# Two-layer transformer kernel: look-up transfers on ScalarE's queue, row marks copied at their own part, two groups of sends released at later parts

## The chip, the cores and the metric

The kernel runs on one core of a Trainium2 chip. The metric is device time in microseconds of one execution of the whole program; lower is better. Engines are named as in the profile: PE (TensorE, matmuls), DVE (VectorE), ACT (ScalarE), POOL (GpSimd), SP (SyncE, which here only issues DMAs).

## The reference, cut to what matters

Two layers are computed on 2 x 1024 tokens of width 512, all in float32: attention, a mixture of experts, a state-space layer and a feed-forward layer, each added to its input after a layer norm.

```
x = x + attention(layernorm(x))              # 16 heads
x = x + experts(layernorm(x))                # 32 experts, the best 8 of each token
x = x + state_space(layernorm(x))            # 16 heads, chunks of 64
x = x + look_up_ffn(layernorm(x))            # weights = lut[idx], 16 values

# experts, for every token t and each of its 8 experts e, with weight masked_w[t, e]:
h   = silu(x[t] @ w_gate[e].T) * (x[t] @ w_up[e].T)        # 192 wide
out[t] += masked_w[t, e] * (h @ w_down[e].T)

# look_up_ffn: gate_idx, up_idx [1376, 512], down_idx [512, 1376], integers 0 to 15
w = lut[idx]                                                # for each of the three
```

The change lies where the experts are computed. The look-up `w = lut[idx]` of the last layer's weights is done beside them.

## The kernel before, in words

**Routing and sends.** Every token's row (512 normalised values, its token number, and its 32 expert weights: `ROW` = 545 floats) is written once for each of its 8 experts into a table `rows` in HBM, at a place that belongs to the expert. A write is an indirect DMA on POOL of 128 rows (`send`, L296). Place k (0 to 7) of a token is its k-th expert, counted from the highest number down. Tokens of the first batch are sent during attention. Of the second batch some places are sent as soon as they are routed; the others come in groups, `send(k)` for place k: 2 DMAs for k = 1, 8 for each k from 2 to 7. Such a send also waits for the latest silu `self.first` of the experts (L1090).

**Parts.** The experts are done from number 31 down to 0, each in two parts: a front part (2 blocks of 128 rows) and a back part (3 blocks, which hold rows of the second batch too). The list `order` has the 64 parts: fronts of n = 0, 1, 2, backs of 0 and 1 (parts 3 and 4), and then front n, back n - 1 in turn (part 5 is front 3, part 6 back 2, part 7 front 4, and so on). `part(p)` writes the instructions of one part, with four yields:

1. `load_weights`, then `gates(p, 0)` (8 matmuls and a silu on ACT), then `begin_turn(p + 1)`;
2. `turn_block` 0 and 1 of part p + 1 (transposes of its rows, copied by ACT to `xgT`), then `down(p - 1)`;
3. `gates(p, 1)` (8 matmuls, a product `hT` on DVE);
4. `turn_block` 2 of part p + 1 (back parts only), `gates(p, 2)` (8 matmuls, silu on ACT, products `hU` on DVE), and `load_rows(p + 3)`.

`begin_turn(p + 1)` has the two copies of the row marks on DVE, L1060 and L1061: `rw` (the rows' weights for this expert) and `tok` (their token numbers), both with four buffers and both read from the rows `xg` (three buffers). They are used in `down`: ACT scales a block of the result by `rw` into `y` (L1140, six buffers), and POOL adds it to `acc` in HBM with an accumulating indirect DMA at the rows `tok` (L1142). `acc` has two halves, used in turn, and accumulations into the same half are kept in order.

**Look-up.** `_look_up` is a generator. It handles 27 pieces of 128 x 688 or 128 x 512 indices. For a piece, `load` fetches it (L921, issued on SP, two buffers), ACT casts it to bf16 (`shorten`, L926), and DVE goes through 16 steps: a compare (L942) and a multiply-add into `acc` (L943; step 0 is one instruction, L937). This `acc` is a tile of the look-up with two buffers, not the table of the experts. The next piece is loaded at step 1 and cast at step 14; the result is stored at step 15 (L951, issued on SP). One `next(look_up)` does one step. From part 5 on, `rest` calls it after each yield of a part: 6 steps in a front part, 9 in a back part.

**What sets the order.** PE, DVE and ACT run in the order in which the program is written (`manual_schedule`). The queues of POOL and SP are ordered by the framework's planner, from this order and its estimates. Each queue is issued in order, so an instruction that waits holds what is behind it.

**Where sends are released.** `rest` issues `send(0)` (empty), `send(1)` and `send(2)` before its loop, `send(3)` in part 2, and `send(4)` to `send(7)` in parts 5, 7, 9 and 11, each after the part's first yield.

Of the kernel before, what the change touches and what calls it, by code (L numbers as in the profile page):

```python
# [32 lines left out]
E, I, TOPK = 32, 192, 8  # L33
# [24 lines left out]
FI, NLUT = 1376, 16  # L58
# [264 lines left out]
def _after(tc, later, earlier, kind=mybir.DependencyClass.Sync):  # L323
    tc.add_manual_dep(
        later.ins, earlier.ins.name, mybir.DependencyInfo(kind, mybir.DependencyReason.DATA)
    )


def _attention(tc, g, x_sb, a, router, gates, load_gates, make_experts):
# [14 lines left out]
    with ExitStack() as ctx:  # L344
# [462 lines left out]
        def group(i, beside, sending):  # L807
# [49 lines left out]
            first, second = (fold(i + 1, hf) if follows else iter(()) for hf in range(2))  # L857
            next(first, None)
            next(ahead, None)
            run(first)  # L860
            next(second, None)
            one(len(blocks) - 1)
            for _ in range(2):
                next(ahead, None)
            run(second)
            run(ahead)
            next(division, None)

# [34 lines left out]
def _look_up(tc, g, a, pool, lut, ffn_w):  # L903

    nc = tc.nc
    half = FI // 2
    pieces = []
    for src, dst in (("gidx", "wg"), ("uidx", "wu")):  # L910
        for cc in range(NCC):
            for hf in range(2):
                cols = slice(hf * half, (hf + 1) * half)
                pieces.append((P, half, a[src][:, cc, cols], ffn_w[dst][:, cc, cols]))
    for fc in range(NFC - 1):
        pieces.append((P, D, a["didx"][:, fc, :], ffn_w["wd"][:, fc, :]))
    pieces.append((FTAIL, D, a["didx_tail"], ffn_w["wd_tail"]))

    def load(n, width, src, dst):
        idx = pool.tile([P, half], I32, tag="idx", name="idx", bufs=2)[:n, :width]  # L920
        nc.sync.dma_start(out=idx, in_=src)  # L921
        return idx

    def shorten(idx, n, width, src, dst):
        short = pool.tile([P, half], BF16, tag="short", name="short", bufs=2)[:n, :width]
        nc.scalar.copy(short, idx)  # L926
        return short

    idx = load(*pieces[0])
    yield  # L930
    short = shorten(idx, *pieces[0])
    for i, (n, width, src, dst) in enumerate(pieces):
        more = pieces[i + 1 : i + 2]
        acc = pool.tile([P, half], F32, tag="acc", name="acc", bufs=2)[:n, :width]
        for k in range(NLUT):
            if k == 0:
                nc.vector.tensor_scalar(  # L937
                    acc, short, float(k), lut[:n, k : k + 1], ALU.is_equal, ALU.mult
                )
            else:  # L940
                hit = pool.tile([P, half], BF16, tag="hit", name="hit", bufs=2)[:n, :width]
                nc.vector.tensor_scalar(hit, short, float(k), None, ALU.is_equal)  # L942
                nc.vector.scalar_tensor_tensor(  # L943
                    acc, hit, lut[:n, k : k + 1], acc, ALU.mult, ALU.add
                )
            if k == 1 and more:
                idx = load(*more[0])
            if k == NLUT - 2 and more:
                ahead = shorten(idx, *more[0])
            if k == NLUT - 1:  # L950
                nc.sync.dma_start(out=dst, in_=acc)  # L951
            yield
        if more:
            short = ahead


def _expert_gates(tc, a, loaded):
# [23 lines left out]
class _Experts:  # L981
# [70 lines left out]
    def begin_turn(self, p):  # L1052
        if p >= len(self.order):
            return
        nc, n, xg = self.tc.nc, self.blocks(p), self.xg[p]
        most = CAPB - FRONTB
        xgT = self.wk.tile([P, NCC, most * P], F32, tag="xgT", name="xgT", bufs=2)
        tok = self.wk.tile([P, most], U32, tag="tok", name="tok", bufs=4)[:, :n]
        rw = self.wk.tile([P, most], F32, tag="rw", name="rw", bufs=4)[:, :n]
        nc.vector.tensor_copy(rw, xg[:, :, D + 1 + self.expert(p)])  # L1060
        nc.vector.tensor_copy(tok, xg[:, :, D])  # L1061
        self.turned[p] = xgT, tok, rw

    def turn_block(self, p, j):
        if p >= len(self.order) or j >= self.blocks(p):
# [83 lines left out]
    def part(self, p):  # L1149

        back = self.order[p - 1] if p else (0, 0)
        if back[1]:
            self.load_weights(back[0] + 3)
        self.gates(p, 0)
        self.begin_turn(p + 1)
        yield
        for j in range(2):
            self.turn_block(p + 1, j)
        self.down(p - 1)
        yield  # L1160
        self.gates(p, 1)
        yield
        self.turn_block(p + 1, 2)
        self.gates(p, 2)
        self.load_rows(p + 3)
        yield

    def ahead(self):

        for n in range(2):  # L1170
            self.load_rows(n)
            self.load_weights(n)
        self.load_rows(2)
        self.load_weights(2)
        yield
        self.begin_turn(0)
        for j in range(2):
            self.turn_block(0, j)
        yield
        for p in range(2):  # L1180
            back = self.order[p]
            self.gates(p, 0)
            self.begin_turn(p + 1)
            yield
            for j in range(2):
                self.turn_block(p + 1, j)
            self.down(p - 1)
            yield
            self.gates(p, 1)
            yield  # L1190
            self.gates(p, 2)
            yield

    def rest(self, sends, fetch):

        tc, a = self.tc, self.a
        nc = tc.nc
        with ExitStack() as ctx:
            def pool(name, bufs, space=None):
                kw = {} if space is None else {"space": space}  # L1200
                return ctx.enter_context(
                    tc.tile_pool(name=name, bufs=bufs, reuse_waits="tile", **kw)
                )

            self.banks = {
                "g": (pool("se_ps_g", 2, PSUM), "g", 2),
                "t": (pool("se_ps_t", 2, PSUM), "t", 2),
                "o": (pool("se_ps_o", 2, PSUM), "o", 2),
                "m": (pool("se_ps_m", 1, PSUM), "m", 1),
            }  # L1210
            lk = pool("se_lk", 1)
            self.both = True

            def send(k):
                for routed, places in sends:
                    if places == [k]:
                        for _ in self.router.send(routed, places, self.first):
                            pass

            for k in range(3):  # L1220
                send(k)
            for p in (3, 4):
                self.load_rows(p)
            look_up = _look_up(tc, self.g, a, lk, self.g["lut"], self.ffn_w)
            next(look_up)
            for p in range(2, len(self.order)):
                n, back = self.order[p]
                for i, _ in enumerate(self.part(p)):
                    if i == 0 and not back and n + 1 < TOPK:

                        send(n + 1)
                    if p > 4:
                        for _ in range(1 + back + (i < 1 + (not back))):
                            next(look_up, None)
                if back and n >= TOPK:
                    got = next(fetch, None)
                    if got:
                        _after(tc, got, self.first)
            self.down(len(self.order) - 1)
            for _ in chain(look_up, fetch):  # L1240
                pass
# [718 lines left out]
```

## Time and profile before

| | |
|---|---|
| median of 3 runs | 2810.66 us (2804.3 to 2813.29) |
| profiled execution | 2820.1 us, its span 2818.4 us |
| mean granted TensorE clock | 0.982 |
| busy, share of the span | PE 96%, DVE 51%, ACT 33%, POOL 23% |
| DMA | 316 MB, mean 112 GB/s |
| experts with the look-up beside them | about 866 to 1535 us of the span |

The times in the trace are microseconds from the start of the span of the one profiled execution, on one core. A row of the timeline has the start, the duration, the engine, the line of the kernel, the operation, `out<-in` by the program's names with shapes, a count, and in brackets the idle time before it and what ended it. Busy time of an engine leaves out instructions that issue DMAs. A wait is put down to the releaser that came last by the profile.

### The profile page before, as it was taken

The numbers are of one execution on the slowest core, as the hardware profiler recorded it, in microseconds if no ns is written. First come the engines' busy times: TensorE is split into PE (matmuls) and PEld (weight loads), VectorE is DVE, ScalarE is ACT, GpSimd is POOL, SyncE is SP. The second block draws the span as 40 slices with busy tenths as digits, with TensorE's granted clock in tenths as the row PEclk, the third lists the DMA queues.
The fourth block names the chain that finished last, engine by engine and source line by source line (L and its number), as shares of the span: only waits on it lengthen the run. The fifth ranks groups of instructions, "written<-read, shape, count | busy, mean of one in ns | idle before, by whom it ended". The sixth has DMA issues, their size and how long they took to land. (4 is left out here: it accounts for less than half of the span.)

```text
span 2818.4 us, 34644 instructions
## 1 busy us (share of the span) xinstructions
PE 2703.1 (96%) x11976; PEld 1624.1 (58%) x11976; DVE 1425.4 (51%) x3952; ACT 933.1 (33%) x1887; POOL 635.7 (23%) x787
## 2 busy tenths in 40 slices
PE   7999999998989899999999699999999999999999
PEld 3444444544465566666665587777777775444444
DVE  5555543655236788987775344554455453101100
ACT  1344432443323233333333333443444433101010
POOL 2222220433355634333333000110111010000000
PEclk9999999998989999999999799999999999999999
DMA  3376532212479999998886301111111140100000
GB/s 115 111 199 184 164 115 70 92 60 74 153 247 248 241 228 255 263 240 202 205 205 107 84 16 36 38 41 44 28 47 42 35 147 20 34 8 27 30 0 26
DMA packets 242793, 315.60 MB, mean 112 GB/s; under 512 B 60753, under 2 KB 129361, under 8 KB 241841
## 3 DMA queue, kind: packets, MB, share of 16 engines
q1 hardware_dynamic: 208320, 234.87, 28.0%
q0 software_dynamic: 33280, 77.68, 13.1%
q8 instruction: 98, 1.61, 0.2%
q10 hardware_dynamic: 1008, 0.73, 0.1%
q14 instruction: 87, 0.70, 0.1%
HBM read 160.17 MB, written 153.04 MB: 111 GB/s over the span
## 5 line engine op out<-in xcount | busy, mean ns | idle before, releaser
L1080 PE MATMUL pg<-xgT,wgu 128*128 128x256 f32 (+1 forms) x1536 | 447.2, 444 | 13.8 <-DVE hT L1093 12.7
L1080 PEld LDWEIGHTS pg<-xgT,wgu 128*128 128x128 f32 x1536 | 289.0, 194 | 161.1 <-issue 51.2
L1142 POOL DMA_INDIRECT acc<-y,tok x160 | 272.9, 1706 | 401.8 <-ACT y L1140 186.7
L943 DVE SCALAR_TENSOR_TENSOR acc<-hit,lut,acc 128x688 f32<-128x688 bf16 (+2 forms) x405 | 348.8, 861 | 14.4
L1443 PE MATMUL pf<-xT,win 128*128 128x256 f32 x1024 | 242.5, 385 | 5.5 <-ACT gate L1471 3.8
L653 ACT ACTIVATE pT<-st 128x512 f32<-128x512 f32 (+3 forms) x384 | 158.7, 497 | 180.6 <-PE st L640 158.0
L548 PE MATMUL sp<-ka,qa 64*128 64x512 f32 (+3 forms) x768 | 207.3, 511 | 8.1 <-DVE mx L569 4.0
L1443 PEld LDWEIGHTS pf<-xT,win 128*128 128x128 f32 x1024 | 187.0, 190 | 38.8 <-PE pf L1443 7.2
L640 PE MATMUL st<-qa,ka 64*128 64x512 f32 (+3 forms) x768 | 182.4, 512 | 2.3 <-issue 1.5
L569 DVE TENSOR_REDUCE mx<-sp 128x1 f32<-128x384 f32 (+3 forms) x352 | 167.3, 492 | 17.4 <-PE sp L548 10.7
L657 POOL TENSOR_SCALAR_AFFINE_SELECT pT<-pT 128x128 f32<-128x128 f32 x256 | 83.5, 338 | 390.2 <-ACT pT L653 378.3
L296 POOL DMA_INDIRECT rows<-row,idx x128 | 128.7, 1005 | 108.3 <-DVE chosen L282 43.6
L1750 PE MATMUL po<-wd,f_hT 128*128 128x512 f32 (+1 forms) x352 | 152.6, 592 | 0.0
L671 PE MATMUL y<-pT,v 128*64 128x512 f32 (+3 forms) x768 | 145.7, 512 | 4.6 <-ACT raw L608 3.1
L562 DVE CUSTOM_DVE_ANT_0 junk<-sp,cmask 128x128 f32<-128x128 f32 x256 | 73.3, 286 | 145.3 <-PE sp L548 135.4
L548 PEld LDWEIGHTS sp<-ka,qa 64*128 64x128 f32 x768 | 91.8, 187 | 93.5 <-issue 49.7
L1694 DVE TENSOR_TENSOR f_hT<-s,pu 128x512 f32<-128x512 f32 (+1 forms) x37 | 25.5, 688 | 232.8 <-PE pu L1688 232.8
L640 PEld LDWEIGHTS st<-qa,ka 64*128 64x128 f32 x768 | 102.3, 192 | 63.2 <-issue 36.9
L1515 POOL TENSOR_TENSOR cd<-ft_c,ec 128x256 f32<-128x256 f32 x56 | 40.8, 730 | 413.3 <-PE cb L1529 205.2
L1140 ACT ACTIVATE y<-yo,rw 128x512 f32<-128x512 f32 x128 | 81.2, 684 | 157.9 <-PE yo L1133 150.1
L1443 PE MATMUL pf<-xT,wc 128*128 128x256 f32 x512 | 125.0, 391 | 8.8 <-DVE ft_b L1462 5.2
L1688 PE MATMUL pg<-f_xT,wg 128*128 128x512 f32 (+1 forms) x296 | 133.4, 593 | 0.0
(213 smaller groups left out, 4034.3 us busy)
## 6 DMA issues: line engine op xcount, KB each, us to landing
rows<-blank SPq DMA_DIRECT2D x160, 272.5 KB
xg<-rows SPq DMA_DIRECT2D x32, 817.5 KB
xg<-rows SPq DMA_DIRECT2D x32, 545.0 KB
csb<-cs_rows SPq DMA_DIRECT2D x128, 128.0 KB
wgu<-in_wg_dram SPq DMA_DIRECT2D x32, 256.0 KB
wgu<-in_wu_dram SPq DMA_DIRECT2D x32, 256.0 KB
wd<-in_wd_dram SPq DMA_DIRECT2D x32, 256.0 KB
wd<-in_wd_dram SPq DMA_DIRECT2D x64, 128.0 KB
```

The source lines that it names most:

```text
L296: t = tc.nc.gpsimd.indirect_dma_start(out=self.rows[:, :], out_offset=bass.IndirectOffsetOnAxis(ap=idx[:, i, k : k + 1], axis=0), in_=xr[i ...
L548: nc.tensor.matmul(sp[hh][:, c0:c1], lhsT=q[half, pr, tb * P : (tb + 1) * P], rhs=k[half, pr, k0 * P : k1 * P], start=True, stop=True,)
L569: nc.vector.tensor_reduce(m[:, n : n + 1], sp[hh][:, c0:c1], AX.X, ALU.max)
L640: nc.tensor.matmul(st[:, c0:], lhsT=k[half, j // 2, kb * P : (kb + 1) * P], rhs=q[half, j // 2, qt * 512 + c0 : (qt + 1) * 512], start=Tru ...
L653: e = nc.scalar.activation(pT[:, c0:], st[:, c0:], AF.Exp)
L671: nc.tensor.matmul(y[j // 2][half, c0:], lhsT=v[:, kb, h // 2, h % 2 : h % 2 + 2, :].rearrange("p k d -> p (k d)"), rhs=ps[j][:, c0:], sta ...
L943: nc.vector.scalar_tensor_tensor(acc, hit, lut[:n, k : k + 1], acc, ALU.mult, ALU.add)
L1080: nc.tensor.matmul(pg, lhsT=wgu[:, cc, m * P : (m + 1) * P], rhs=xgT[:, cc, :cols], start=cc == 0, stop=cc == NCC - 1,)
L1142: nc.gpsimd.indirect_dma_start(out=self.router.acc[to][:, :], out_offset=bass.IndirectOffsetOnAxis(ap=tok[:, j : j + 1], axis=0), in_=y, i ...
L1443: nc.tensor.matmul(pf, lhsT=w[wn][:, cc, c0 : c0 + P], rhs=xT[st][:, cc], start=cc == 0, stop=cc == NCC - 1,)
L1688: nc.tensor.matmul(dst[:n, :], lhsT=w[:, cc, fc * P : fc * P + n], rhs=self.xT[tt][:, cc, :], start=cc == 0, stop=cc == NCC - 1,)
L1750: nc.tensor.matmul(po, lhsT=self.hT[tt][fc // 4][:n, fc % 4, j * P : (j + 1) * P], rhs=wd[:n, fc, :], start=fc == 0, stop=fc == NFC - 1,)
```

## The change

Three things are changed, all in the experts' stage. (a) The loads and stores of the look-up are issued on ACT's queue instead of SP's, and a piece is stored at step 4 of the next piece instead of at its own last step; the last piece is stored after one more yield. (b) The two copies of the row marks leave `begin_turn(p + 1)` for a function `marks(p)` that `part(p)` and `ahead` call just before `begin_turn(p + 1)`; so the marks of a part are copied in its own part, not in the part before. (c) `send(2)` moves from before the loop to part 2, and `send(3)` from part 2 to part 3; `send(4)` to `send(7)` stay.

```diff
 def _look_up(tc, g, a, pool, lut, ffn_w):
     def load(n, width, src, dst):
         idx = pool.tile([P, half], I32, tag="idx", name="idx", bufs=2)[:n, :width]
-        nc.sync.dma_start(out=idx, in_=src)
+        nc.scalar.dma_start(out=idx, in_=src)
         return idx
...
+    done = None
     for i, (n, width, src, dst) in enumerate(pieces):
...
             if k == NLUT - 2 and more:
                 ahead = shorten(idx, *more[0])
-            if k == NLUT - 1:
-                nc.sync.dma_start(out=dst, in_=acc)
+            if k == 4 and done:
+                nc.scalar.dma_start(out=done[0], in_=done[1])
             yield
+        done = dst, acc
         if more:
             short = ahead
+    yield
+    nc.scalar.dma_start(out=done[0], in_=done[1])
...
     def begin_turn(self, p):
         if p >= len(self.order):
             return
-        nc, n, xg = self.tc.nc, self.blocks(p), self.xg[p]
+        n = self.blocks(p)
         most = CAPB - FRONTB
         xgT = self.wk.tile([P, NCC, most * P], F32, tag="xgT", name="xgT", bufs=2)
         tok = self.wk.tile([P, most], U32, tag="tok", name="tok", bufs=4)[:, :n]
         rw = self.wk.tile([P, most], F32, tag="rw", name="rw", bufs=4)[:, :n]
+        self.turned[p] = xgT, tok, rw
+
+    def marks(self, p):
+        nc, n, xg = self.tc.nc, self.blocks(p), self.xg[p]
+        _, tok, rw = self.turned[p]
         nc.vector.tensor_copy(rw, xg[:, :, D + 1 + self.expert(p)])
         nc.vector.tensor_copy(tok, xg[:, :, D])
-        self.turned[p] = xgT, tok, rw
...
         self.gates(p, 0)                 # in part(p), and alike in ahead()
+        self.marks(p)
         self.begin_turn(p + 1)
...
-            for k in range(3):
+            for k in range(2):
                 send(k)
...
                 for i, _ in enumerate(self.part(p)):
-                    if i == 0 and not back and n + 1 < TOPK:
-                        send(n + 1)
+                    if i == 0 and (p < 4 or not back) and n + (p > 4) < TOPK:
+                        send(p if p < 4 else n + 1)
```

More of the change, by code (lines that the diff above doesn't have):

```diff
@@ L1182, in ahead @@
             self.gates(p, 0)
+            self.marks(p)
             self.begin_turn(p + 1)
```

## The prediction

> **What bounds the kernel now.** I read the page first (PE busy 96% of the span), then the waits of PE, to see where the missing time lies, then the busy time by stage, and at last the timeline of the stage that the change touches. The routed experts run from about 788 to 1548 us; the look-up runs beside them from 866 us on. From 865 to 1500 us PE waits for two things only (waits of PE; columns: us in total, times, longest):
>
> ```profile
> PE pg L1080 <- DVE hT L1093: 12.7, 3, 6.4
> PE pg L1080 <- DVE acc L943: 1.1, 1, 1.1
> ```
>
> So the gates matmuls wait for VectorE, four times. The stages (busy time by window; the last columns are granted clock, DMA share, GB/s) put all of it before 1000 us:
>
> ```profile
> 865.00:1000.00 135.00, 121.18 (x478) 75.91 (x477) 102.72 (x200) 42.15 (x78) 79.76 (x58) 0.95 0.95 245
> 1000.00:1500.00 500.00, 500.00 (x2063) 319.63 (x2062) 414.58 (x873) 179.88 (x334) 191.93 (x112) 1.00 0.92 226
> 924.00:931.00 7.00, 5.72 (x11) 3.22 (x12) 6.73 (x15) 0.17 (x1) 5.47 (x6) 0.52 1.00 331
> 979.00:986.00 7.00, 4.57 (x8) 2.64 (x9) 6.73 (x15) 0.00 (x0) 4.08 (x3) 0.52 0.97 179
> ```
>
> After 1000 us PE never waits, and 135.0 - 121.2 = 13.8 us of waiting lie in 865 to 1000. Behind the two long stalls the granted clock is 0.52. Why VectorE is late, its own waits in the same stretch say:
>
> ```profile
> DVE tok L1061 <- DMA acc<-y,tok: 18.6, 4, 6.9
> ```
>
> It stands at the cast of `tok` until an accumulating scatter (L1142) has let go of a `tok` buffer. The timeline shows the four casts, and PE behind the two long ones (behind the others it waits 1.10 us at 898.06 and 1.68 at 952.43):
>
> ```profile
> 892.82 0.17 DVE L1061 CAST tok<-xg 128x3 uint32<-128x3 f32 x1 [2.46 <-DMA acc<-y,tok]
> ...
> 920.35 0.17 DVE L1061 CAST tok<-xg 128x3 uint32<-128x3 f32 x1 [6.17 <-DMA acc<-y,tok]
> ...
> 925.28 5.46 PE L1080 MATMUL pg<-xgT,wgu 128*128 128x384 f32 x8 [4.64 <-DVE hT L1093]
> ...
> 947.43 0.17 DVE L1061 CAST tok<-xg 128x3 uint32<-128x3 f32 x1 [3.02 <-DMA acc<-y,tok]
> ...
> 975.69 0.17 DVE L1061 CAST tok<-xg 128x3 uint32<-128x3 f32 x1 [6.93 <-DMA acc<-y,tok]
> ...
> 981.43 4.95 PE L1080 MATMUL pg<-xgT,wgu 128*128 128x384 f32 x8 [6.41 <-DVE hT L1093]
> ```
>
> Which scatter each waits for, the queue of GpSimd tells (the first and third scatter of part 6, the second and third of part 10; the first of part 8 is issued at 933.83):
>
> ```profile
> 906.60 1.61 POOL L1142 DMA_INDIRECT acc<-y,tok  x1 [0.30 <-issue]
> ...
> 912.34 1.87 POOL L1142 DMA_INDIRECT acc<-y,tok  x1 [1.57 <-ACT s L1090]
> ...
> 963.71 1.74 POOL L1142 DMA_INDIRECT acc<-y,tok  x1 [0.30 <-issue]
> ...
> 967.50 1.64 POOL L1142 DMA_INDIRECT acc<-y,tok  x1 [2.06 <-ACT xgT L1071]
> ```
>
> Four buffers: the cast for part p+1, made in part p, takes the buffer of part p-3. In parts 7, 9, 11 and 13 that is a back part with three scatters, the last issued at 912.34 for the cast that ends at 920.35, at 967.50 for 975.69: about 8.1 us from issue to release. From 906.60 to 933.83 one pair of parts takes GpSimd 27.2 us, of which its eight sends (L296) are 10.4 (895.94 to 906.30 in the pair before); PE needs 22.35 (silus L1090 at 1019.55, 1041.90, 1064.25). GpSimd falls back 4.9 us a pair as long as sends last (parts 5, 7, 9, 11), and the four `tok` buffers are what makes PE wait for it.
>
> **What goes.** (1) The marks are written one part later, in a buffer of part p-4. The number of instructions stays (two of 0.16 us a part); the allowed lag grows by one part, 10.7 to 11.7 us (silus L1090 at 888.01 to 877.27, and 1053.5 to 1041.9). The waits were 2.46, 6.17, 3.02 and 6.93 us, each shorter than that. Worth, if nothing follows: stalls 1.10 + 4.64 + 1.68 + 6.41 = 13.8; slowed clock, 5.46 - 2.82 and 4.95 - 2.82 us for the eight matmuls and 1.32 - 1.04 for the transposes behind the first, 5.1; together 18.9 us.
>
> (2) What is late next. `y` has six buffers for five scatters a pair, so a `y` takes the buffer of the scatter six before. GpSimd's chain does not shorten: it is in order, and a scatter waits for the one two before it (same `acc` half: 906.60 to 912.34, 5.7 us). The third `y` of part 12 (ScalarE, 971.69 in part 13) needs the scatter of 963.71. Release takes 5.7 us by that spacing, 8.1 by the casts; I take 5.8, as this scatter has fewer ahead of it, so 969.5: part 13 can be at most 2.2 us ahead of today when it gets there. What the first three stalls gave is then taken back except 2.2 us; part 13's own stall and slow clock, 6.41 + 2.13 = 8.5 us, come after that `y` and are saved. Sum 10.7. Then part 14's marks would stand at 983.69 - 10.7 = 973.0, while the scatter that they wait for is released at 975.69: VectorE waits 2.7 us, of which PE has felt 0.5 to 1.5 us less in the four cases, so 1.2 to 2.2 back at most. I take 10; bounds from this item 6 (release 8.1 us, and all of the 2.7 felt) and 18.9.
>
> (3) Send 3 moves from part 2 to part 3, send 2 from before part 2 into it. Send 2 waits for part 2's silu (821.51), when GpSimd is still at earlier ones: nothing. Send 3's eight (10.4 us) leave the place before the scatters of part 1 (842.23) and go into GpSimd's gaps of 3.9, 6.0 and 2.7 us between 846 and 865: 12.6 us for 10.4, so send 4 begins 0 to 2 us later than at 867.04. Rows of expert parts that need sends 2 and 3 are fetched at 838.40 and 854.44 and used 20 us or more later. Cost 0 to 2, taken 0.
>
> (4) Look-up on ScalarE's queue: 27 loads and 27 stores. SP issues a load in 0.33 to 2.33 us; ScalarE's own issues at the start of the kernel took 0.40 to 0.45. So 54 x 0.45 = 24 us in 640 us, beside an ScalarE that is 36% busy (179.88 of 500). The tightest place is before the copy of the third turned block, which PE needs within some 1 us; ScalarE idles 0.95 us there (1049.16), and the 0.77 us cast of `short` stood there at 1025.73 with no wait of PE. A 0.45 us issue is covered. If each issue took 2.33 us, those in that place (3 of 15 steps a pair, so 11 of 54) would cost 1.4 us each, 15 us; I take 0, and 0 to 4 into the range.
>
> A store is issued at step 4 of the next piece, five steps (5 x 1.27 us, a 0.33 us compare and a 0.94 us multiply-add) behind the last write of `acc`, so it finds it done unless VectorE is 6.4 us behind ScalarE. The `acc` buffer is needed again 11 steps later, 14 us.
>
> (5) SP loses 54 issues and the waits at stores (21.8 us from 800 to 1000 us), behind which weights and rows were queued. But rows for part p+3 can now be fetched only after part p's marks: 872.91 becomes some 878, 883.55 some 889. They are used two parts after the marks, 22 us, and landing took 6.9 us (818.55 to 825.41). Covered; the weights behind them on SP are needed a pair later. Nothing gained either: no wait of PE after 865 us is for SP's transfers.
>
> (6) Two stalls before 865 us stay: 4.11 us at 825.52 (rows of part 3, whose sends do not move) and 3.69 us at 847.72, where ScalarE was held 7.4 us by something that the trace does not name. They may move by up to 4 us either way.
>
> **Sum.** 10 us of the 18.9 stay saved; items 3 to 6 add nothing. The profiled run took 2820.1 us (span 2818.4), 9.4 above the median; I carry the difference over: 2810.7 - 10 = 2800.7 us.
>
> **Rivals.** *B, the lag is never caught.* If GpSimd's chain is 8 us shorter by part 13, say because scatters there release in 5.7 us all along, the `y` buffers are always free and the whole 18.9 us go: 2791.8, and 2788 if the 3.7 us at 847 go as well. For it: the 5.7 us link above. Against: the next link (912.34 to 921.05) took 8.7, at a DMA share of 0.95. 0.22.
>
> *C, a third queue slows the scatters.* The 16 DMA engines are 0.95 busy at 245 GB/s. Load and store of a piece, 0.69 MB every 24 us, now come as a stream of their own; if three streams share alike, that stream is in flight 0.69 MB / 82 GB/s = 8.4 us of 27.2, and a scatter in that time gets a third where it had half, 1.5 times as long. The scatters on the chain take 14.4 us a pair (906.60 to 921.05), so 0.5 x 0.31 x 14.4 = 2.2 us a pair, 8.9 in four: the gain shrinks to 1, 2809.6. Against: the same bytes moved before, in front of the same engines. 0.15. [...] No trace before shows ScalarE's queue at work beside the others in this stage.
>
> *D, the stores hold ScalarE: slower.* ScalarE is in order; while it stands at a store for `acc`, the silus and copies behind it stand too, then PE. It decides from a lag of VectorE of 6.4 us + 1 us of cover. At 9.4 us each store holds 3 us, 27 x 2 - 10 = 44 us more, 2855; 8.4 us slower begins at 1.7 us a hold. Against: after 1000 us VectorE starts a part at most 2.2 us behind the silu (1021.7 and 1019.5). 0.08.
>
> **Chances.** 0.3%, 8.4 us, is about what a measurement of this kernel can tell from no change. Forecast (6 to 14 us gained) 0.50, of it 0.33 beyond 8.4; B 0.22; C 0.15; D 0.08; 0.05 for other orders of SP's and GpSimd's queues, which no list in the kernel fixes. Faster 0.33 + 0.22 + 0.03 = 0.58, same 0.17 + 0.13 = 0.30, slower 0.12. The range goes from B's deep end, 2788, to just above C, 2812; D and half of the rest are left out. The forecast's own range is 2796 to 2805.
>
> **What would show it.** Right: no wait of VectorE at `tok` in parts 7, 9, 11; a wait of ScalarE's `y` for a scatter in parts 11 to 13; PE's idle time from 865 to 1000 down from 13.8 to about 6 us; one slow-clock stretch instead of two. Scatters released later than 8.1 us after issue speak for C; ScalarE waiting at its stores, for D; none of these and no idle PE, for B. The step most likely wrong is (2).

## The result, and the profile after

| | kernel before | changed kernel |
|---|---|---|
| median of 22 runs each | 2811.38 us (2803.11 to 2815.4) | 2804.99 us (2798.49 to 2810.07) |
| ratio to before | | 0.9979 (0.9971 to 0.9987) |
| again, in another session | 2826.18 us | 2818.59 us, ratio 0.9973 (0.9958 to 0.9987) |
| profiled execution, its span | 2820.1, 2818.4 us | 2804.13, 2802.4 us |

The change gains 5.9 us by the first ratio (0.0021 x 2811) and 7.6 by the second: 0.2 to 0.3%, just under what was called measurable. The forecast was 10. The two profiled spans lie 16 us apart, but 9.6 us of that are there before the experts begin (first silu at 788.0 and 778.4), where nothing was changed. So stages are compared from the silu of part 2 on.

The waits of PE from 865 to 1000 us in the changed kernel (us in total, times, longest), then VectorE's at `tok` and ScalarE's at `y`:

```profile
PE pg L1090 <- ACT xgT L1081: 10.2, 3, 3.8
```

```profile
DVE tok L1072 <- DMA acc<-y,tok: 2.0, 3, 1.1
```

```profile
ACT y L1150 <- DMA acc<-y,tok: 15.3, 6, 2.9
```

VectorE's wait at the `tok` cast fell from 18.6 us to 2.0, and in its place ScalarE waits 15.3 us at `y`. PE's waits fell only from 13.8 to 10.2 us, and they are named for `xgT` now: the copy of the third turned block stands behind the two `y` in ScalarE's order.

The same stages as before, and the three places of lowered clock (busy time by window; last columns granted clock, DMA share, GB/s):

```profile
865.00:1000.00 135.00, 124.76 (x479) 76.96 (x478) 106.85 (x206) 42.91 (x79) 79.76 (x55) 0.95 0.95 247
1000.00:1500.00 500.00, 500.00 (x2061) 319.29 (x2061) 413.22 (x878) 178.89 (x333) 196.33 (x113) 1.00 0.95 225
```

```profile
906.00:916.00 10.00, 6.40 (x17) 3.80 (x17) 5.07 (x12) 2.20 (x5) 5.17 (x4) 0.66 1.01 279
939.00:946.00 7.00, 7.00 (x22) 3.54 (x20) 5.70 (x12) 1.57 (x3) 3.67 (x3) 0.76 0.90 218
966.00:973.00 7.00, 6.92 (x20) 3.78 (x20) 6.37 (x15) 1.93 (x5) 3.85 (x3) 0.76 1.00 250
```

After 1000 us PE still never waits. In the clock records the halved clock (0.50) lasts 6.8, 3.4 and 3.4 us at 908.6, 939.3 and 966.6; before it was 6.8 us twice. The sum is 13.6 us in both kernels: two long stalls became three shorter ones, and each still lowers the clock.

Where the three stalls come from, the timelines of ScalarE (`y` that waited), GpSimd (the first two scatters behind each block of sends) and PE show:

```profile
905.14 0.69 ACT L1150 ACTIVATE y<-yo,rw 128x512 f32<-128x512 f32 x1 [2.87 <-DMA acc<-y,tok]
908.45 0.69 ACT L1150 ACTIVATE y<-ym,rw 128x512 f32<-128x512 f32 x1 [2.63 <-DMA acc<-y,tok]
933.61 0.69 ACT L1150 ACTIVATE y<-yo,rw 128x512 f32<-128x512 f32 x1 [2.29 <-DMA acc<-y,tok]
936.79 0.69 ACT L1150 ACTIVATE y<-ym,rw 128x512 f32<-128x512 f32 x1 [2.49 <-DMA acc<-y,tok]
961.05 0.69 ACT L1150 ACTIVATE y<-yo,rw 128x512 f32<-128x512 f32 x1 [2.54 <-DMA acc<-y,tok]
964.21 0.69 ACT L1150 ACTIVATE y<-ym,rw 128x512 f32<-128x512 f32 x1 [2.47 <-DMA acc<-y,tok]
```

```profile
899.58 1.63 POOL L1152 DMA_INDIRECT acc<-y,tok  x1 [0.30 <-issue]
901.51 1.85 POOL L1152 DMA_INDIRECT acc<-y,tok  x1 [0.30 <-issue]
...
927.56 1.61 POOL L1152 DMA_INDIRECT acc<-y,tok  x1 [0.30 <-ACT short L926]
929.47 1.90 POOL L1152 DMA_INDIRECT acc<-y,tok  x1 [0.31 <-issue]
...
955.80 1.66 POOL L1152 DMA_INDIRECT acc<-y,tok  x1 [0.30 <-issue]
957.77 1.96 POOL L1152 DMA_INDIRECT acc<-y,tok  x1 [0.30 <-issue]
```

```profile
909.67 5.49 PE L1090 MATMUL pg<-xgT,wgu 128*128 128x384 f32 x8 [3.60 <-ACT xgT L1081]
...
938.01 4.22 PE L1090 MATMUL pg<-xgT,wgu 128*128 128x384 f32 x8 [2.88 <-ACT xgT L1081]
...
966.08 4.54 PE L1090 MATMUL pg<-xgT,wgu 128*128 128x384 f32 x8 [3.77 <-ACT xgT L1081]
```

ScalarE's `y` takes the buffer of the scatter six before. The `y` at 905.14 goes on 5.6 us after the scatter of 899.58 was issued, that at 908.45 6.9 us after 901.51, and so in each of three pairs of parts.

**The measure for the experiments.** Three rows carry it, two of the kernel before and one of the changed one, whose scatter of 955.80 stands above:

```profile
961.79 1.61 POOL L1142 DMA_INDIRECT acc<-y,tok  x1 [0.30 <-issue]
...
997.19 0.38 ACT L1090 ACTIVATE s<-pg 128x256 f32<-128x256 f32 x1 [1.29 <-DVE hit L942]
```

```profile
981.45 0.38 ACT L1100 ACTIVATE s<-pg 128x256 f32<-128x256 f32 x1 [1.29 <-PE pg L1090]
```

GpSimd's first scatter behind the last sends (961.79 before, 955.80 after) stands for its chain; the silu of part 15 (997.19 and 981.45) is the first behind the stage. The *gap* is their difference, 35.4 us before and 25.6 after: the smaller, the further PE may be ahead of GpSimd. "p5" and "p15" are the silus of parts 5 and 15 counted from that of part 2. "Chain" is the time from the first scatter behind the sends of part 5 (878.14 before) to that behind the last sends, three pairs of parts. Where the sends stand between the scatters ("sends between" and "both"), the last send comes later, and gap and chain are taken at the same two scatters by count, the 10th and the 25th of the experts. "Idle" is PE's idle time from 865 to 1000 us, "half" the time at half clock in the same stretch (records that begin in it). All but the ratio come from one profile each. From the silu of part 15 to the end of the span 13 of the 14 profiles take 1820.7 to 1822.1 us, and that of experiment 5 takes 1818.5, so what sets the kernels apart lies ahead of part 15. The first silu of the experts, which comes before anything that was changed, moves between 778.4 and 792.4 us from profile to profile.

| kernel | ratio to before | p5 | p15 | gap | chain | idle | half |
|---|---|---|---|---|---|---|---|
| before | | 44.1 | 175.7 | 35.4 | 83.7 | 13.8 | 13.6 |
| before, again | 0.9998 (0.9984 to 1.0011) | 49.5 | 178.6 | 35.2 | 81.3 | 11.3 | 13.6 |
| look-up's queue alone | 0.9986 (0.9972 to 1.0) | 47.2 | 176.6 | 33.6 | 83.5 | 11.4 | 10.2 |
| sends alone | 0.9997 (0.9984 to 1.001) | 39.6 | 175.6 | 35.5 | 81.6 | 16.3 | 17.0 |
| changed | 0.9979 (0.9971 to 0.9987) | 40.1 | 169.2 | 25.6 | 85.5 | 10.2 | 13.6 |
| changed, again | 0.9973 (0.9958 to 0.9987) | 40.0 | 166.2 | 27.2 | 82.6 | 9.2 | 10.2 |
| marks alone | 0.9981 (0.9966 to 0.9995) | 46.1 | 172.9 | 27.7 | 86.7 | 9.6 | 13.6 |
| marks and queue | 0.9976 (0.9956 to 0.9996) | 47.1 | 169.8 | 25.7 | 84.6 | 8.6 | 6.8 |
| changed, look-up on SP | 0.9992 (0.9975 to 1.0009) | 40.2 | 166.4 | 27.0 | 84.1 | 11.3 | 6.8 |
| before, 6 `tok` | 0.9994 (0.9976 to 1.0013) | 40.4 | 162.3 | 25.0 | 80.4 | 7.0 | 6.8 |
| changed, sends between | 0.9961 (0.9946 to 0.9976) | 39.9 | 161.7 | 27.8 | 78.9 | 7.6 | 3.4 |
| changed, 8 `y`, 6 `tok` | 0.9965 (0.995 to 0.9979) | 40.2 | 154.5 | 12.4 | 84.1 | 3.4 | 0 |
| before, 8 `y`, 6 `tok` | 0.9950 (0.9931 to 0.9968) | 44.7 | 158.0 | 19.9 | 81.3 | 1.3 | 0 |
| changed, both | 0.9934 (0.9913 to 0.9954) | 43.3 | 157.9 | 22.3 | 77.0 | 4.2 | 0 |

Each ratio is against the kernel before in the same session, whose median was 2811.38 us for the changed kernel's first row, 2822.41 for the three parts alone and marks and queue, 2810.95 for look-up on SP, before with 6 `tok`, sends between and the changed kernel with 8 `y`, and 2826.18 for the rest. The session with 2810.95 ran on another chip than those with 2822.41 and 2826.18.

### The profile page after: what moved, and what is told of

It is laid out like the page before. It is cut to its first block, busy times and chain, and to the rows that moved or that the text cites. A ratio compares the mean times of both kernels' runs of the same rounds, so it can differ in the third digit from the quotient of the medians.

```text
span 2802.4 us, 34613 instructions
## 1 busy us (share of the span) xinstructions
PE 2698.3 (96%) x11976; PEld 1621.7 (58%) x11976; DVE 1423.8 (51%) x3952; ACT 932.2 (33%) x1887; POOL 640.3 (23%) x787
## 3 DMA queue, kind: packets, MB, share of 16 engines
q1 hardware_dynamic: 200608, 217.96, 26.3%
## 5 line engine op out<-in xcount | busy, mean ns | idle before, releaser
L1090 PE MATMUL pg<-xgT,wgu 128*128 128x256 f32 (+1 forms) x1536 | 448.4, 445 | 10.2 <-ACT xgT L1081 10.2
L653 ACT ACTIVATE pT<-st 128x512 f32<-128x512 f32 (+3 forms) x384 | 158.0, 499 | 176.2 <-PE st L640 159.3
L569 DVE TENSOR_REDUCE mx<-sp 128x1 f32<-128x384 f32 (+3 forms) x352 | 167.2, 491 | 17.9 <-PE sp L548 10.7
L1150 ACT ACTIVATE y<-yo,rw 128x512 f32<-128x512 f32 x128 | 81.3, 683 | 166.3 <-PE yo L1143 158.6
L1700 PE MATMUL pu<-f_xT,wu 128*128 128x512 f32 (+1 forms) x296 | 133.2, 592 | 0.0
```

The costliest lines, as they stand in the source:

```text
L569: nc.vector.tensor_reduce(m[:, n : n + 1], sp[hh][:, c0:c1], AX.X, ALU.max)
L653: e = nc.scalar.activation(pT[:, c0:], st[:, c0:], AF.Exp)
L1090: nc.tensor.matmul(pg, lhsT=wgu[:, cc, m * P : (m + 1) * P], rhs=xgT[:, cc, :cols], start=cc == 0, stop=cc == NCC - 1,)
L1700: nc.tensor.matmul(dst[:n, :], lhsT=w[:, cc, fc * P : fc * P + n], rhs=self.xT[tt][:, cc, :], start=cc == 0, stop=cc == NCC - 1,)
```

## The experiments

**1. The marks alone.** From the kernel before, only this:

```diff
         self.gates(p, 0)
+        self.marks(p)
         self.begin_turn(p + 1)
```

> The kernel before with the marks alone copied at their own part. Theory (GpSimd's chain of sends and accumulations sets the pace of parts 5 to 13, and what the change gives is one more part of lead over it): the chain is as before, the lead grows by the 9.8 us seen in the changed kernel, so 8 to 10 us faster than before, with no wait of VectorE at tok and a wait of ScalarE's y for a scatter instead. Rivals (the gain comes from SP's relieved queue, or from the moved sends): no change within 2 us.

Ratio 0.9981, 5.4 us (1.4 to 9.6) for the 8 to 10 expected; gap 27.7 us, 7.7 less than before. The waits at `tok` are 5.4 us, where none was expected, and ScalarE's at `y` 12.5. The marks alone do what the whole change does to the gap, and as much of its gain as these intervals can tell.

**2. The look-up's queue and later store alone.**

```diff
-        nc.sync.dma_start(out=idx, in_=src)
+        nc.scalar.dma_start(out=idx, in_=src)
...
-            if k == NLUT - 1:
-                nc.sync.dma_start(out=dst, in_=acc)
+            if k == 4 and done:
+                nc.scalar.dma_start(out=done[0], in_=done[1])
```

> The kernel before with the look-up's loads and stores alone on ScalarE's queue, stores at step 4 of the next piece. Theory of the chain: within 2 us of before, the four waits of VectorE at tok still there, 15 to 20 us in sum. Rival (SP's relieved queue): about 6 us faster. Rival (a third queue slows the scatters): 2 to 9 us slower, the first scatters of back parts over 28 us apart.

Ratio 0.9986, an interval of no change to 7.9 us gained; the profile shows p15 0.9 us later than before and the waits at `tok` still at 17.2 us, now in seven waits. Where the timed 4 us would come from, no line of this profile shows; its run, 2824.09 us, was 4.7 above the kernel's median. That stays open, and by the time alone the rival of 6 us is not refuted.

**3. The sends alone.**

```diff
-            for k in range(3):
+            for k in range(2):
                 send(k)
...
+                    if i == 0 and (p < 4 or not back) and n + (p > 4) < TOPK:
+                        send(p if p < 4 else n + 1)
```

> The kernel before with the two groups of sends alone released at later parts. Theory of the chain: the chain starts some 1.5 us later and the lead is as before, so 0 to 3 us slower, the waits at tok a little longer. Rival (the gain comes from the early parts, where part 3's silu no longer comes late): 4 to 6 us faster, the silu of part 3 some 16 us behind that of part 2 instead of 24.

Ratio 0.9997, no difference; gap 35.5, chain 81.6. Here part 5 comes 4.5 us earlier than before, and part 15 at the same time (175.6, 175.7): PE idles longer (16.3 us) until GpSimd's chain has caught up. What PE gains ahead of this stage is lost in it. The silu of part 3 comes 17.2 us behind that of part 2, as the rival said, but the moved sends are not shown to be the reason: in experiment 5, with the sends in their old place, it comes after 16.4. What both profiles lack is the hold of ScalarE ahead of the silu at 845.72 in the kernel before.

**4. Marks and queue, sends as before.**

> The changed kernel without the move of the two groups of sends (they are where they were before). Theory of the chain: 1 to 3 us faster than the changed kernel, so 7 to 9 us faster than before, as the chain starts earlier. Rival (the moved sends bring the gain): no faster than before by more than 2 us.

Ratio 0.9976, 6.8 us (1.1 to 12.4): the full change without its third part, and no less gained as far as this interval tells.

**5. A longer lag by other means: two more `tok` buffers.** From the kernel before, marks where they were:

```diff
-        tok = self.wk.tile([P, most], U32, tag="tok", name="tok", bufs=4)[:, :n]
-        rw = self.wk.tile([P, most], F32, tag="rw", name="rw", bufs=4)[:, :n]
+        tok = self.wk.tile([P, most], U32, tag="tok", name="tok", bufs=6)[:, :n]
+        rw = self.wk.tile([P, most], F32, tag="rw", name="rw", bufs=6)[:, :n]
```

> The kernel before with six buffers instead of four for `tok` and `rw`, nothing else. Theory (what the later marks bring is only a longer allowed lag between PE and GpSimd's chain of accumulations): the casts of `tok` in parts 7 to 13 no longer wait, part 15 starts 8 to 10 us earlier against the release of the last slow scatter (35.4 us behind it before), and the time is 4 to 9 us below the kernel before, as with the later marks alone (5.4 measured). Rival (the later place of the marks matters by itself, by what SP or VectorE do there): within 2 us of before.

In the profile the casts do not wait, the gap is 25.0 us, 10.4 less than before, and the same wait comes next (waits of ScalarE, 865 to 1000 us):

```profile
ACT y L1140 <- DMA acc<-y,tok: 12.3, 4, 5.3
```

So by the profile the place of the marks counts for nothing by itself; the lag that it allows does. The time did not show the 4 to 9 us: 0.9994 (0.9976 to 1.0013), the medians 3.8 us apart. This expectation on the time failed, and the profiled run was 12 us below its kernel's median. By the time alone the rival is not refuted.

**6. The look-up on SP's queue again, the rest of the change kept.**

> The changed kernel with the look-up's loads and stores issued by SP again, the stores still five steps later. Theory (the queue that carries the look-up matters neither to GpSimd's chain nor to PE): within 2 us of the changed kernel, the chain's fifth block of scatters at 142 to 145 us behind part 2 as with ScalarE's queue (143.5). Rival (a third queue slows the scatters; 3.2 us of lost gain): the chain stands where it did before, at 140.3, and the time is 3 us below the changed kernel.

Ratio 0.9992 (0.9975 to 1.0009), which can tell neither. The chain's scatter stood at 139.4 us behind part 2, where 142 to 145 was expected: a miss, and the number of the rival. But it does not count for it: the changed kernel, profiled again with ScalarE's queue, has 138.9, and the kernel before, again, 143.3. The number moves by 4 us from run to run.

**7. More `y` buffers.** In the changed kernel:

```diff
-            y = self.wk.tile([P, D], F32, tag="y", name="y", bufs=6)
+            y = self.wk.tile([P, D], F32, tag="y", name="y", bufs=8)
```

and, as in experiment 5, six buffers of `tok` and `rw`; the space comes from one buffer instead of two for the look-up's `idx` and `hit`. What these two cost, and what the `y` buffers give without the others, was not run.

> The changed kernel with eight `y` buffers for six and six of `tok` and `rw` for four (paid for by one buffer for two of the look-up's indices and compares). Theory (the buffers are all that ties PE to GpSimd's chain here): ScalarE's 15.3 us of waits at `y` and PE's 10.2 us at the gates matmuls from 865 to 1000 us go, and with them 13.6 us at half clock, which cost some 5 us; 10 to 15 us below the changed kernel, 16 to 21 below the kernel before. Rival (GpSimd's chain sets the pace by some other tie, such as rows fetched after the sends): 0 to 3 us below the changed kernel.

Waits of PE and the stage, 865 to 1000 us:

```profile
PE xg_ps L1080 <- DMA xg<-rows: 1.8, 1, 1.8
PE pg L1090 <- ACT xgT L1081: 1.6, 1, 1.6
```

```profile
865.00:1000.00 135.00, 131.60 (x541) 83.18 (x540) 123.17 (x230) 48.25 (x88) 79.89 (x58) 1.00 0.99 261
```

The idle time fell to 3.4 us and the granted clock stays at 1.00. The silus of parts 5 to 13 are 22.35 us apart pair by pair (89.4 us for four), as after 1000 us: PE is the bound again. ScalarE still waits 12.4 us at `y`, where none was expected, but now with only 1.6 us of PE's behind it. Part 15 comes 11.7 to 14.7 us earlier than in the two profiles of the changed kernel, as expected. The time is 9.8 us below before (5.9 to 14.1), 16 to 21 expected: a gain over the kernel before is clear, one over the changed kernel (5.9 and 7.6 in other sessions) only by the profiles, and the size is not borne out.

**8. The same buffers in the kernel before.**

> The kernel before with eight `y` buffers and six of `tok` and `rw` (one for two of the look-up's indices and compares), none of the change. Theory (the only part of the change that counts is the lead that it allows, and these buffers allow more): as the changed kernel with the same buffers, 9 to 16 us below the kernel before, part 15 starting 12 to 16 us behind the fifth block of scatters. Rival (the look-up's queue, its later stores or the moved sends bring a part of their own that longer leads uncover): 4 us or more above the changed kernel with these buffers.

```profile
PE pg L1080 <- ACT xgT L1071: 1.3, 1, 1.3
```

```profile
865.00:1000.00 135.00, 133.66 (x551) 85.04 (x550) 117.68 (x224) 48.47 (x90) 78.22 (x60) 1.00 0.97 267
```

Ratio 0.9950, 14.1 us (9.0 to 19.5). Without any part of the change it gains no less than with it. From part 5 to part 13 it takes 89.4 us, as experiment 7 does. The gap, 19.9 us, missed its 12 to 16: once nothing holds PE, the gap only tells when PE entered the stage and how fast GpSimd was. Against part 2, part 15 is 3.5 us later here than in experiment 7 and GpSimd's scatter 4.0 earlier.

**9. A shorter chain: sends 4 to 7 between the scatters.** In the changed kernel, `send` only queues its 8 DMAs, and `down` takes two after each scatter (`later(k)`, left out here, hands out the DMAs of group k one by one):

```diff
...
             self.turn += 1
+            for _ in range(2):
+                next(self.waiting, None)
...
-                        send(p if p < 4 else n + 1)
+                        if p < 4:
+                            send(p)
+                        else:
+                            self.waiting = chain(self.waiting, later(n + 1))
```

> The changed kernel with the sends 4 to 7 not issued eight in a row but two behind each accumulating scatter. Theory (GpSimd's chain is sends and scatters in turn, each scatter waiting for the one two before it, 5.7 to 8.7 us, while the 1.3 us sends stand in a block of their own): the sends go into the time in which a scatter waits, a pair of parts takes the chain 20 to 23 us instead of 28, PE does not wait from 865 to 1000 us, and the time is 8 to 15 us below the changed kernel. Rival (the 16 DMA engines, 0.95 busy, set the pace, and the sends' bytes take the same time wherever they stand): within 2 us of the changed kernel.

GpSimd's timeline of one pair of parts:

```profile
894.53 1.57 POOL L1153 DMA_INDIRECT acc<-y,tok  x1 [0.30 <-issue]
901.71 1.89 POOL L1153 DMA_INDIRECT acc<-y,tok  x1 [5.62 <-issue]
903.90 0.99 POOL L296 DMA_INDIRECT rows<-row,idx  x1 [0.30 <-issue]
905.20 1.04 POOL L296 DMA_INDIRECT rows<-row,idx  x1 [0.30 <-issue]
906.55 1.61 POOL L1153 DMA_INDIRECT acc<-y,tok  x1 [0.30 <-ACT s L1108]
908.81 2.38 POOL L1153 DMA_INDIRECT acc<-y,tok  x1 [0.64 <-issue]
911.49 1.45 POOL L296 DMA_INDIRECT rows<-row,idx  x1 [0.30 <-issue]
...
```

The queue took its sends two in one place and six in another. Two cover one wait (906.55 follows at once), one wait of 5.6 us stays, and a pair takes 26.3 us (78.9 / 3) where 20 to 23 was expected. That is still above PE's 22.35, and PE waits 7.6 us. The ratio, 0.9961, is 11.0 us below before (6.7 to 15.2), less than the 14 to 23 that the expectation comes to; that it is faster than the change is not shown by this interval, in which its 7.6 us lie.

**10. Both.**

> The changed kernel with both: eight `y` buffers and six of `tok` and `rw`, and the sends 4 to 7 issued two behind each accumulating scatter. Theory (the buffers allow PE a longer lead over GpSimd's chain, the other order shortens the chain; what is left to win is the 1.6 us at the gates and 1.8 us at fetched rows that the buffers alone left): within 4 us of the changed kernel with the buffers alone, 9 to 16 us below the kernel before. Rival (the two gains add up): 18 us or more below the kernel before.

Ratio 0.9934, 18.7 us (13.0 to 24.6) below before, the fastest here; beside it, in the same session, before with the buffers alone is 3.2 us slower by the medians. The chain takes 77.0 us, yet part 15 comes no earlier than with buffers alone (157.9, against 154.5 and 158.0), and parts 5 to 13 take the same 89.4 us. So the profile speaks for the theory and the time, at the edge, for the rival; what the shorter chain adds to the buffers is not settled.

**11 and 12. Both kernels again**, for what a single profile is worth.

> The kernel before, unchanged, profiled and timed a second time, on the chip of the runs beside it. Theory (the 7.4 us hold of ScalarE ahead of the silu at 845.72, and the later start of the experts, 788.0 against 778.4 us, belong to single runs and not to the kernel): in this profile one or both are missing, and the 33 to 36 us by which part 15 starts behind the fifth block of scatters are there again, with PE's waits of 11 to 15 us between 865 and 1000 us. Rival (they belong to the kernel before, and the change took them away): both are there again. The time: a ratio of 1 within 0.0015.

> The changed kernel, unchanged, profiled and timed a second time on the same chip as the kernel before. Theory: 4 to 9 us below the kernel before; part 15 starts 24 to 28 us behind the fifth block of scatters, and the chain takes 83 to 87 us from the second block to the fifth, as before. Rival (a chain that the change makes slower): 86 us or more from the second block to the fifth, beside 83 or less in the kernel before.

ScalarE's waits from 780 to 900 us, in before again and in changed again:

```profile
ACT s L1097 <- remote: 10.7, 1, 10.7
```

```profile
ACT s L1107 <- remote: 14.1, 2, 10.9
```

The unnamed hold of ScalarE (7.4 us in the first profile of before) is in both kernels here, and in none of the four profiled in the session with 2810.95 us, one of which (experiment 5) is the kernel before but for its buffers. It does not belong to the change: the theory's "missing" did not come true, and both marks are there again, as the rival said, but the hold in the changed kernel too, so the rival falls as well. Whether it goes with the chip is open. The first silu of the experts is at 790.2 and 790.7, so the 9.6 us between the first two profiles do not belong to it either. The gaps came back, 35.2 and 27.2; the chain takes 81.3 and 82.6 us.

## Why the prediction was right or wrong

**The time.** 2800.7 was forecast, 2804.99 measured: inside the range, at the upper end of the forecast's own 2796 to 2805. That is in part luck: the range, 2788 to 2812, holds the unchanged kernel's 2811.38 as well, and of the two measured gains 5.9 us lies just below the 6 to 14 that were forecast and 7.6 inside. The largest chance was on a gain of over 0.3%; it is 0.2 to 0.3%.

**(1) The allowed lag: right.** Waits at `tok` fell from 18.6 to 2.0 us; the two more buffers of experiment 5 shorten the gap alike without moving an instruction. Over all profiles, the four with four `tok` buffers and the old place have gaps of 33.6 to 35.5 (mean 34.9), the six with a longer lag and six `y`, sends in their block, 25.0 to 27.7 (mean 26.4): 8.6 us, where 10 was taken.

**(2) What is late next: right wait, wrong place and size.** It is the six `y` buffers and GpSimd's in-order scatters; with eight of them (and six `tok`) parts 5 to 13 go at PE's own pace. But the step let that wait bite once, in part 13, and counted part 13's own stall and slow clock (8.5 us) as saved in full. It bites in three pairs of parts, because a lead won early meets the same ring early, and part 13 keeps a stall of 3.77 us and 3.4 us at half clock. Two terms were mis-sized. The release of the scatter in question was taken as 5.8 us: at the second scatter of a block it measured 6.9, 7.3 and 6.4 (908.45 - 901.51, 936.79 - 929.47, 964.21 - 957.77), mean 6.9, so the sum of 10.7 loses 1.1 (0.6 by the last, which is the scatter that was meant). And PE's idle time was to fall to some 6 us with one slow stretch: it is 10.2 and 9.2 us, and the half clock lasts 13.6 and 10.2 us, against 13.6.

Between the 8.6 us of the gap and the timed 5.9 and 7.6 some 1 to 3 us are missing; of the other four kernels with the longer lag, those of experiments 1 and 4 gained 5.4 and 6.8 us and those of experiments 5 and 6 only 1.7 and 2.2, in a session in which the kernel before was not profiled. The chain was taken as unchanged. Its scatter stands 3.2 us later in the first pair of profiles (143.5, 140.3) and 4.4 earlier in the second (138.9, 143.3); its length averages 82.5 us in the four profiles without the longer lag and 84.0 in the six with it, spread over 2.4 and 6.2 us. A delay of about that size could hide there; it is not shown.

**(3) to (5): taken at nothing, and borne out within the intervals.** The sends alone change nothing. ScalarE issues the look-up's 54 transfers in 0.33 to 0.39 us each but one (0.77), mostly less than the 0.45 taken, and PE never waits after 1000 us.

**Rival D** does not occur: each of the 27 stores is issued 1.5 to 13.4 us after the end of VectorE's last write of its `acc`, so none waits for it. One of them, 0.08 us behind the start of a silu in ScalarE's timeline:

```profile
915.24 0.49 ACT L1100 ACTIVATE s<-pg 128x384 f32<-128x384 f32 x1 [5.23 <-issue]
915.32 0.33 ACTq L953 DMA_DIRECT2D f_wg<-acc  x1
```

**(6)** The two early stalls did move, by run rather than by kernel, and experiment 3 shows that it would not have mattered: the stage behind takes it back.

**Rival B** fell: the chain did catch PE; its sign, no wait that holds PE for the chain, comes only with eight `y`. **Rival C** named a third queue that slows the scatters. Four profiles with ScalarE's queue and six `y`, sends in their block, have chains of 82.6 to 85.5 us, six on SP's 80.4 to 86.7. No slowing of 2.2 us a pair (6.6 in the chain's three) shows. The 2.2 us rested on three streams that share the engines alike; no run shows that share, and these chains are what the runs showed in its place.

## What to carry to other kernels

An in-order chain on one engine, tied to another by several rings of buffers, gives back what a longer ring wins once the next ring binds (here 18.6 us of waits at `tok` fell to 2.0, and 15.3 us came at `y`): before costing the removal of a wait, list every ring between the two engines with its reach in time, and lengthen those that bind together. A stall saved ahead of a stage that another engine paces was worth nothing here (experiment 3: part 5 came 4.5 us earlier, part 15 at the same time); measure such a stage by the distance between the two engines at its end. Profile both kernels twice before a few microseconds of one stage are explained: here holds of 7 to 14 us came and went between runs of the same kernel.

## What the runs showed of the hardware

**The granted clock.** From 815 to 1010 us it stands at 1.00 or 0.50 in the profiles of both kernels. In the changed kernel it is 0.50 for 3.4 us from 816.45, for 6.8 us from 908.61, and for 3.4 us each from 939.33 and 966.64, at PE's stalls of 3.89, 3.60, 2.88 and 3.77 us that end at 816.07, 909.67, 938.01 and 966.08. In the kernel before it is 0.50 for 3.4 us from 825.30 and for 6.8 us each from 924.28 and 978.90, at the stalls of 4.11, 4.64 and 6.41 us that end at 825.52, 925.28 and 981.43; at those of 1.10, 1.68 and 3.69 us (ending at 898.06, 952.43 and 847.72) it stays at 1.00. So the length of a stall alone does not tell its slow clock: 3.60 us cost twice the time at 0.50 that 3.77 did, and 3.69 cost none. What decides it was not shown. In all, from 865 to 1000 us, three stalls of 3 to 4 us cost as much slow clock, 13.6 us, as two of 5 and 6.

A transfer of the look-up issued from ScalarE took it 0.33 to 0.39 us, one of the 54 took 0.77. An accumulating scatter of 128 rows of 2 KB was released 5.3 to 7.3 us after its issue in the changed kernel (the six that a `y` waited for, 899.58 to 957.77), at a DMA share of 0.95.
